# Two-layer graph attention on one core: filling order of a two-bank accumulator, a paired last sum, and a moved transpose

## The chip, the core and the metric

The kernel runs on one core of a Trainium2 chip. The metric is the device time of one execution in microseconds (us), as the median of several runs. TensorE (PE) does the matrix multiplications and the transposes, VectorE (DVE) and ScalarE (ACT) the elementwise work, GpSimd (POOL) one addition per block, and SyncE (SP) issues all transfers.

## The reference

For each of 32 graphs of 512 nodes, a layer norm and a ReLU are followed by two graph attention layers, and their result is added to the input:

```python
h = jnp.maximum(_layernorm(x, axis=-1), 0.0)
x = x + gnn(adj, h, ...)

def gat_layer(x, mask, W, a_src, a_dst, bias, concat):
    xl = (x @ W).reshape(B, N, H, F)
    asrc = jnp.einsum('bnhf,hf->bnh', xl, a_src)
    adst = jnp.einsum('bnhf,hf->bnh', xl, a_dst)
    e = leaky_relu(asrc[:, :, None, :] + adst[:, None, :, :], 0.2)
    e = jnp.where(mask[..., None], e, NEG_INF)
    attn = softmax(e, axis=1)
    out = jnp.einsum('bsdh,bshf->bdhf', attn, xl)
```

Layer 1 has 4 heads of 256 features (joined, with bias and ELU behind them), layer 2 has one head of 512. Everything is float32 but the masks. x is (32, 512, 512), adj (32, 512, 512) int32.

## The kernel before, in words

The 512 nodes of a graph are four blocks of 128 rows. The order of TensorE's instructions is the order of the program (`manual_schedule` for PE); the other engines' instructions are put in order by a list scheduler, which takes what it believes ready, by place in the program. Each engine then runs its own list strictly in that order.

One pass of the main loop (index `i`) takes four stages on TensorE, each on another graph:

- `project1(i+1)`: x @ W1, eight accumulators `pxl` of two banks (L279 to L287), each copied out by ACT (L286). Between them stand `turned_masks` (L177, L180), and, behind the fourth and fifth accumulator, layer 1's `columns` and `rows` for heads 0 and 1.
- `gather2(i-1)`: the last sum of layer 2 (L350 to L366): for each of four blocks `d` a load of x, an addition of the bias by POOL (L356), four matmuls into one bank of `ps` (L360), an addition by DVE (L364) and a store (L365). Two blocks share a two-bank accumulator.
- `project2(i)`: h1 @ W2, four accumulators `pxm` (L331, L338).
- `gather1(i+1)`: the weighted sums of layer 1 (L294 to L313): for each head `h` one accumulator `po` of two banks, `ps[:, f, :]` with `f` 0 and 1. Each half takes four matmuls (L301) and is then evicted: ACT exp (L308), DVE min (L309), DVE bias and max (L310). The half is evicted before the next half is filled.

All these accumulators share one ring of three two-bank buffers (tag "mm", bufs=3). Transposes use another ring of two (tag "tp").

The softmax of a head is the class `Soft`: `columns` copies its columns; `rows` turns them on TensorE (`pas`, L196) and spreads them over all partitions by two transfers through DRAM (L200, L202); `first` makes the row sums (ACT L232, DVE L235, ACT L239, ACT L242, and DVE L243 to L246, which write `r`); `turn` does for `r` what `rows` does for the columns (`prr`, L196, L200, L202); `second` makes the weights `p` (DVE L261, ACT L265, DVE L269). Layer 1 has four such chains; a table `plan` says behind which step of `gather2` and `project2` each part is issued. Layer 2's chain is called `late`. Before, its `rows` and `first` are issued behind the first half of `gather1`, its `turn` behind the sixth half, and its `second` behind the first accumulator of the next `project1`.

In the traces one matmul of float32 shows as two records, so a half of `po` is 8 records, `gather1` 64 and `gather2` 32.

Of the kernel before, what the change touches and what calls it, by code (L numbers as in the profile page):

```python
# [8 lines left out]
F32 = mybir.dt.float32  # L9
# [3 lines left out]
OP = mybir.AluOpType  # L13
# [3 lines left out]
P = 128  # L17
# [11 lines left out]
def tile_gat(  # L29
# [23 lines left out]
    nc = tc.nc  # L53
    B, N, D = x.shape
    H, FH = as1.shape
    HF = H * FH
    DO = w2.shape[1]
    NT = N // P
    KT = D // P
    FT = HF // P  # L60
    FPH = FH // P
# [4 lines left out]
    work = ctx.enter_context(tc.tile_pool(name="work", bufs=2))  # L66
    psum = ctx.enter_context(tc.tile_pool(name="psum", bufs=1, space=PSUM))
# [18 lines left out]
    b2_sb = const.tile([P, DO], F32, name="b2_sb")  # L86
# [36 lines left out]
    def load(b):  # L123
        XT[b] = []
        for t in range(NT):
            xt = work.tile([P, D], F32, tag="x", name=f"x{b}_{t}", bufs=4)
            nc.sync.dma_start(xt, x[b, t * P : (t + 1) * P, :])
            XT[b].append(xt)

    def load_adj(b):  # L130
        ADJ[b] = []
        for t in range(NT):
            a = work.tile([P, N], I32, tag="adj", name=f"adj{b}_{t}", bufs=2)
            nc.sync.dma_start(a, adj[b, t * P : (t + 1) * P, :])
            ADJ[b].append(a)

    def norm(b):

        stats = work.tile([P, NT, nc.vector.BN_STATS_DIM], F32, tag="stats", name=f"stats{b}")
        mv = work.tile([P, NT, nc.vector.BN_AGGR_DIM], F32, tag="mv", name=f"mv{b}")  # L140
        for t in range(NT):
            nc.vector.bn_stats(stats[:, t, :], XT[b][t])  # L142
            nc.vector.bn_aggr(mv[:, t, :], stats[:, t, :])
        rstd = work.tile([P, NT], F32, tag="rstd", name=f"rstd{b}")
        nc.vector.tensor_scalar_add(rstd, mv[:, :, 1], EPS)
        nc.gpsimd.tensor_tensor(rstd, rstd, half, op=OP.pow)
        yield
        HT[b] = work.tile([P, KT, N], F32, tag="ht", name=f"ht{b}", bufs=1)
        for t in range(NT):
            hn = work.tile([P, D], F32, tag="hn", name=f"hn{b}_{t}")  # L150
            nc.vector.tensor_scalar(  # L151
                hn, XT[b][t], mv[:, t, 0:1], rstd[:, t : t + 1], op0=OP.subtract, op1=OP.mult
            )
            ps = psum.tile([P, KT, P], F32, tag="tp", name=f"pht{b}_{t}", bufs=2)
            for k in range(KT):
                nc.tensor.transpose(ps[:, k, :], hn[:, k * P : (k + 1) * P], identf)
            nc.scalar.activation(HT[b][:, :, t * P : (t + 1) * P], ps, AF.Relu)
            yield
        del XT[b]
# [134 lines left out]
    def gather1(b):  # L294
        H1[b] = work.tile([P, FT, N], F32, tag="h1", name=f"h1{b}", bufs=1)
        for h in range(H):
            p = PS1.pop((b, h))
            ps = psum.tile([P, 2, 512], F32, tag="mm", name=f"po{b}_{h}", bufs=3)
            for f in range(FPH):
                for s in range(NT):  # L300
                    nc.tensor.matmul(  # L301
                        ps[:, f, :], xl[:, s, h, 2 + f * P : 2 + (f + 1) * P], p[:, s, :],
                        start=(s == 0), stop=(s == NT - 1),
                    )
                g = h * FPH + f
                bias = b1_sb[:, g : g + 1]
                e = work.tile([P, N], F32, tag="et", name=f"e{b}_{g}", bufs=2)
                nc.scalar.activation(e, ps[:, f, :], AF.Exp, bias=bias)  # L308
                nc.vector.tensor_scalar(e, e, 1.0, -1.0, op0=OP.min, op1=OP.add)  # L309
                nc.vector.scalar_tensor_tensor(  # L310
                    H1[b][:, g, :], ps[:, f, :], bias, e, op0=OP.add, op1=OP.max
                )
                yield  # L313

    def x2(b):

        if b < B - 1:
            return xl2

        return bass.AP(  # L320
            tensor=xl.tensor, offset=xl.offset, ap=[xl.ap[0], [DO + 2, NT], [1, DO + 2]]
        )
# [27 lines left out]
    def gather2(b):  # L350
        p = PS2.pop(b)
        v = x2(b)
        for d in range(NT):
            xr = work.tile([P, D], F32, tag="xr", name=f"xr{b}_{d}", bufs=3)
            nc.sync.dma_start(xr, x[b, d * P : (d + 1) * P, :])
            nc.gpsimd.tensor_tensor(xr, xr, b2_sb, op=OP.add)  # L356
            if d % 2 == 0:
                ps = psum.tile([P, 2, 512], F32, tag="mm", name=f"po2{b}_{d}", bufs=3)
            for s in range(NT):
                nc.tensor.matmul(  # L360
                    ps[:, d % 2, :], p[:, s, d * P : (d + 1) * P], v[:, s, 1 : DO + 1],
                    start=(s == 0), stop=(s == NT - 1),
                )
            nc.vector.tensor_tensor(xr, ps[:, d % 2, :], xr, op=OP.add)  # L364
            nc.sync.dma_start(out[b, d * P : (d + 1) * P, :], xr)  # L365
            yield  # L366

    def step(g):

        if g is not None:  # L370
            next(g, None)

    def rest(g):
        for _ in g or ():
            pass
# [7 lines left out]
    late = None  # L383
    with tc.manual_schedule(engines={mybir.EngineType.PE}):
        for i in range(-1, B + 1):

            front = i + 2 < B
            nm = norm(i + 2) if front else None
            if front:
                load(i + 2)  # L390
                load_adj(i + 2)
                step(nm)
            s1 = None
            if i + 1 < B:
                s1 = Soft(i + 1, 1, cols1, lambda h, p, b=i + 1: PS1.__setitem__((b, h), p))
                mt = turned_masks(i + 1)
                for n, _ in enumerate(project1(i + 1)):
                    if n == 0 and late:
                        late.second(0)
                    step(mt)  # L400
                    if n == 3:
                        s1.columns(0)
                    if n == 4:
                        s1.rows(0)
                    if n == 5:
                        s1.first(0)
                    if n == 7:
                        s1.columns(1)
                        s1.first(1)
            elif late:  # L410
                late.second(0)
            late = None
            last = i == B - 1
            stages = [gather2(i - 1)] if i >= 1 else []
            if 0 <= i < B:
                stages.insert(0 if last else 1, project2(i))

            plan = {
                1: lambda: s1.rows(1),
                3: lambda: (s1.turn(0), s1.first(2)),  # L420
                4: lambda: s1.second(0),
                6: lambda: (s1.turn(1), s1.first(3)),
                7: lambda: s1.second(1),
                8: lambda: s1.turn(2),
                9: lambda: s1.second(2),
                10: lambda: s1.turn(3),
                11: lambda: s1.second(3),
            }
            n = 0
            for g in stages:  # L430
                for _ in g:
                    n += 1
                    if s1 and n in plan:
                        plan.pop(n)()
                    if n in (2, 5, 7, 9):
                        step(nm)
                    if last and n == 8:
                        late = Soft(i, 2, cols2(i), lambda h, p, b=i: PS2.__setitem__(b, p))
                        late.columns(0)
                        late.rows(0)  # L440
                        late.first(0)
                    if last and n == 12:
                        late.turn(0)
            if s1:
                for n in sorted(plan):
                    plan.pop(n)()
            rest(nm)
            if 0 <= i < B and not last:
                late = Soft(i, 2, cols2(i), lambda h, p, b=i: PS2.__setitem__(b, p))
                late.columns(0)  # L450
            if i + 1 < B:
                for n, _ in enumerate(gather1(i + 1)):
                    if n == 0 and late:
                        late.rows(0)
                        late.first(0)
                    if n == 5 and late:
                        late.turn(0)
                    if n == 4 and front:
                        masks(i + 2)

# [28 lines left out]
```

## Time and profile before

| | before |
|---|---|
| median of 3 runs | 4053.54 us (4049.14 to 4060.91) |
| the profiled execution: its time, its span | 4057.44 us, 4055.7 us |
| PE busy | 3482.1 us (86%) |
| DVE busy | 2075.8 us (51%) |
| ACT busy | 1754.1 us (43%) |
| POOL busy | 230.0 us (6%) |
| mean granted TensorE clock | 0.936 of full speed |

Times in the rows below are microseconds from the start of the span, where a row begins with a time. A row of a timeline has the start, the duration, the engine, the line, the operation, what it writes and reads, and in brackets the idle time of the engine before it with what ended it.

### The profile page before, as it was taken

Reading aid. Unit: us, or ns where it says so; the run is one execution under the profiler, and the core shown is the slowest. Engines: PE = TensorE matmul, PEld = TensorE weight load, DVE = VectorE, ACT = ScalarE, POOL = GpSimd, SP = SyncE. Lnnn points to the kernel's source line nnn. Section 1 sums busy time; section 2 is a strip of 40 time slices with the busy share of each in tenths; the row PEclk is TensorE's granted clock in tenths of the full one; section 3 lists DMA queues with packets and bytes.
Section 4 is the critical chain, followed back from the end, with each engine's and each line's share of the span. In section 5 each row is a group of like instructions: output and inputs, shape, how many; then the busy total and the mean of one; then the engine's idle time right before and its main releaser. Section 6 shows DMA issues by size and latency. Waiting matters only on the chain.

```text
span 4055.7 us, 35993 instructions
## 1 busy us (share of the span) xinstructions
PE 3482.1 (86%) x12544; PEld 2278.3 (56%) x12544; DVE 2075.8 (51%) x4739; ACT 1754.1 (43%) x3489; POOL 230.0 (6%) x166
## 2 busy tenths in 40 slices
PE   4888889888889888898888988888988889888887
PEld 3655556555566455665555665546645556555564
DVE  7454555445554455554455544555544555445452
ACT  4443444443444335444344444344443444434451
POOL 0000000000000000000000000000000000000000
PEclk7999999999899899999999999999999999989999
DMA  5121222111222112221122221122211222111111
GB/s 166 34 69 48 75 67 81 65 58 55 70 76 71 50 57 70 76 79 58 47 76 66 81 69 64 50 65 76 79 57 47 73 68 81 63 46 59 60 55 47
DMA packets 120390, 269.41 MB, mean 66 GB/s; under 512 B 15504, under 2 KB 20496, under 8 KB 120208
## 3 DMA queue, kind: packets, MB, share of 16 engines
q1 hardware_dynamic: 120208, 267.12, 20.3%
q8 instruction: 98, 1.61, 0.2%
q14 instruction: 84, 0.69, 0.1%
HBM read 232.53 MB, written 34.54 MB: 66 GB/s over the span
## 4 chain that ended last, share of the span: by engine, by line
PE 45%; DVE 25%; ACT 15%; DMA 12%; issue 2%; POOL 1%; SPq 0%; DVEq 0%; POOLq 0%; ACTq 0%
PE po L301 22%; PE pxl L282 16%; DVE p L261 7%; DVE p L269 6%; ACT l L239 6%; PE po L360 5%; ACT l L232 5%; DMA oas<-das 4%; DMA orr<-drr 4%; DVE l L235 3%; DVE h L310 2%; DMA x<-in_x_dram 2%; ACT e L308 2%; DVE xr L364 1%; DVE hn L151 1%
## 5 line engine op out<-in xcount | busy, mean ns | idle before, releaser
L301 PE MATMUL po<-p,xl 128*128 128x512 f32 x2048 | 1109.5, 699 | 345.2 <-DVE h L310 345.2
L301 PEld LDWEIGHTS po<-p,xl 128*128 128x128 f32 x2048 | 444.0, 224 | 964.5 <-issue 528.8
L282 PE MATMUL pxl<-w_sb,ht 128*128 128x258 f32 x4096 | 931.8, 384 | 2.4 <-DMA adj<-in_adj_dram 1.6
L331 PE MATMUL pxm<-w_sb,h 128*128 128x257 f32 x4096 | 920.9, 379 | 0.0
L282 PEld LDWEIGHTS pxl<-w_sb,ht 128*128 128x128 f32 x4096 | 767.0, 190 | 126.5 <-issue 14.8
L331 PEld LDWEIGHTS pxm<-w_sb,h 128*128 128x128 f32 x4096 | 761.5, 189 | 130.1 <-issue 11.1
L235 DVE CUSTOM_DVE_ANT_0 l<-l,mt 128x512 f32<-128x512 f32 x640 | 432.1, 703 | 383.3 <-ACT l L232 383.3
L265 ACT ACTIVATE p<-p,lo 128x512 f32<-128x512 f32 x640 | 426.3, 716 | 450.7 <-DVE p L261 450.7
L308 ACT ACTIVATE e<-po,b_sb 128x512 f32<-128x512 f32 x256 | 174.9, 683 | 891.0 <-PE po L301 891.0
L360 PE MATMUL po<-xl,p 128*128 128x512 f32 x1024 | 472.7, 604 | 83.3 <-DVE xr L364 71.5
L239 ACT ACTIVATE l<-l,low 128x512 f32<-128x512 f32 x640 | 454.2, 711 | 87.4 <-DVE low L235 86.8
L232 ACT ACTIVATE l<-oas,sc 128x512 f32<-128x512 f32 x640 | 426.6, 710 | 97.5 <-DMA oas<-das 97.5
L261 DVE SCALAR_TENSOR_TENSOR p<-orr,lo 128x512 f32<-128x512 f32 x640 | 442.0, 752 | 49.4 <-DMA orr<-drr 49.4
L309 DVE TENSOR_SCALAR e<-e 128x512 f32<-128x512 f32 x256 | 108.7, 425 | 644.6 <-ACT e L308 644.6
L286 ACT ACTIVATE xl<-pxl 128x516 f32<-128x516 f32 x256 | 151.3, 597 | 612.8 <-PE pxl L282 612.6
L269 DVE TENSOR_TENSOR p<-p,m 128x1024 f32<-128x1024 f32 x320 | 402.2, 1275 | 4.9 <-ACT p L265 4.7
L356 POOL TENSOR_TENSOR xr<-xr,b_sb 128x512 f32<-128x512 f32 x128 | 196.7, 1537 | 3453.4 <-DMA xr<-in_x_dram 2858.1
L360 PEld LDWEIGHTS po<-xl,p 128*128 128x128 f32 x1024 | 188.4, 191 | 314.7 <-issue 201.3
L310 DVE SCALAR_TENSOR_TENSOR h<-po,b_sb,e 128x512 f32<-128x512 f32 x256 | 191.3, 747 | 5.9
L180 DVE TENSOR_SCALAR mt<-pm 128x512 bf16<-128x512 bf16 x128 | 54.3, 424 | 267.3 <-PE pm L177 267.3
L142 DVE BATCH_NORM_STATS2 stats<-x 128x6 f32<-128x512 f32 x128 | 87.4, 684 | 129.5 <-DMA x<-in_x_dram 129.5
L198 DVE COPY rrr<-prr 8x128 f32<-8x128 f32 x160 | 43.4, 271 | 162.5 <-PE prr L196 162.5
(43 smaller groups left out, 1174.9 us busy)
## 6 DMA issues: line engine op xcount, KB each, us to landing
orr<-drr SPq DMA_DIRECT2D x160, 512.0 KB
x<-in_x_dram SPq DMA_DIRECT2D x128, 256.0 KB
adj<-in_adj_dram SPq DMA_DIRECT2D x128, 256.0 KB
xr<-in_x_dram SPq DMA_DIRECT2D x128, 256.0 KB
oas<-das SPq DMA_DIRECT2D x64, 512.0 KB
out_dram<-xr SPq DMA_DIRECT2D x128, 256.0 KB
oas<-das SPq DMA_DIRECT2D x32, 256.0 KB
drr<-rrr SPq DMA_DIRECT2D x160, 4.0 KB
```

Of the source, the lines that this page charges most:

```text
L232: nc.scalar.activation(e, self.asr[i][:, j, :], AF.Prelu, bias=ad[:, d : d + 1], alpha=SLOPE)
L235: nc.vector.tensor_tensor_reduce(out=e, in0=e, in1=MASKT[self.b][:, d, :], scale=-1.0, scalar=BIG, op0=OP.add, op1=OP.min, accum_out=low[: ...
L239: nc.scalar.activation(e, e, AF.Exp, bias=low[:, d : d + 1], scale=-1.0, accum_out=tot[:, d : d + 1])
L261: nc.vector.scalar_tensor_tensor(p[:, u, :], rr[:, 0, :], lo[:, 0, j, u : u + 1], rr[:, 1, :], op0=OP.add, op1=OP.max,)
L265: nc.scalar.activation(p[:, u, :], p[:, u, :], AF.Exp, bias=lo[:, 1, j, u : u + 1])
L269: nc.vector.tensor_tensor(pp, pp, MASK[self.b][:, t : t + 2, :], op=OP.min)
L282: nc.tensor.matmul(ps[:, j, :W], ht[:, k, t * P : (t + 1) * P], w1_sb[:, k, hp + j, :], start=(k == 0), stop=(k == KT - 1),)
L301: nc.tensor.matmul(ps[:, f, :], xl[:, s, h, 2 + f * P : 2 + (f + 1) * P], p[:, s, :], start=(s == 0), stop=(s == NT - 1),)
L308: nc.scalar.activation(e, ps[:, f, :], AF.Exp, bias=bias)
L310: nc.vector.scalar_tensor_tensor(H1[b][:, g, :], ps[:, f, :], bias, e, op0=OP.add, op1=OP.max)
L331: nc.tensor.matmul(ps[:, j, : W - 1], h1[:, k, t * P : (t + 1) * P], w2_sb[:, k, j * (W - 1) : (j + 1) * (W - 1)], start=(k == 0), stop=(k ...
L360: nc.tensor.matmul(ps[:, d % 2, :], p[:, s, d * P : (d + 1) * P], v[:, s, 1 : DO + 1], start=(s == 0), stop=(s == NT - 1),)
```

## The change

Three things are altered. In `gather1` both halves of a head are filled first, and then both are evicted; a step of the loop (`yield`) still stands behind each half. In `gather2` two blocks share one load tile (two buffers of two blocks, in place of three of one), one POOL addition over both, one DVE addition over both, and two stores behind it. In layer 2's chain, `rows` and `first` are issued behind the third half of `gather1` (step 2) instead of the first, and `turn` behind the first accumulator of the next `project1`, right before `second`, instead of behind the sixth half of `gather1`.

```diff
@@ gather1
                     )
+                if f < FPH - 1:
+                    yield
+            for f in range(FPH):
                 g = h * FPH + f
...
                 )
-                yield
+            yield
@@ gather2
-        for d in range(NT):
-            xr = work.tile([P, D], F32, tag="xr", name=f"xr{b}_{d}", bufs=3)
-            nc.sync.dma_start(xr, x[b, d * P : (d + 1) * P, :])
-            nc.gpsimd.tensor_tensor(xr, xr, b2_sb, op=OP.add)
-            if d % 2 == 0:
-                ps = psum.tile([P, 2, 512], F32, tag="mm", name=f"po2{b}_{d}", bufs=3)
-            for s in range(NT):
-                nc.tensor.matmul(
-                    ps[:, d % 2, :], p[:, s, d * P : (d + 1) * P], v[:, s, 1 : DO + 1],
-                    start=(s == 0), stop=(s == NT - 1),
-                )
-            nc.vector.tensor_tensor(xr, ps[:, d % 2, :], xr, op=OP.add)
-            nc.sync.dma_start(out[b, d * P : (d + 1) * P, :], xr)
+        for d in range(0, NT, 2):
+            xr = work.tile([P, 2, D], F32, tag="xr", name=f"xr{b}_{d}", bufs=2)
+            for j in range(2):
+                nc.sync.dma_start(xr[:, j, :], x[b, (d + j) * P : (d + j + 1) * P, :])
+            nc.gpsimd.tensor_tensor(
+                xr, xr, b2_sb[:, None, :].to_broadcast([P, 2, D]), op=OP.add
+            )
+            ps = psum.tile([P, 2, 512], F32, tag="mm", name=f"po2{b}_{d}", bufs=3)
+            for j in range(2):
+                for s in range(NT):
+                    nc.tensor.matmul(
+                        ps[:, j, :], p[:, s, (d + j) * P : (d + j + 1) * P], v[:, s, 1 : DO + 1],
+                        start=(s == 0), stop=(s == NT - 1),
+                    )
+                if j == 0:
+                    yield
+            nc.vector.tensor_tensor(xr, ps, xr, op=OP.add)
+            for j in range(2):
+                nc.sync.dma_start(out[b, (d + j) * P : (d + j + 1) * P, :], xr[:, j, :])
             yield
@@ main loop, project1
                     if n == 0 and late:
+                        late.turn(0)
                         late.second(0)
...
             elif late:
+                if i < B:
+                    late.turn(0)
                 late.second(0)
@@ main loop, gather1
-                    if n == 0 and late:
+                    if n == 2 and late:
                         late.rows(0)
                         late.first(0)
-                    if n == 5 and late:
-                        late.turn(0)
```

## Rows read from the trace of the kernel before

**Rows 1.** Stages of one pass: length, PE, PEld, DVE, ACT, POOL busy, clock, DMA, GB/s.

```profile
1993.83:2022.90 29.07, 29.07 (x146) 25.04 (x145) 8.83 (x24) 9.25 (x18) 0.00 (x0) 1.00 0.18 55
2022.90:2039.77 16.87, 14.94 (x39) 6.46 (x38) 10.28 (x35) 13.58 (x32) 3.32 (x2) 1.00 0.38 129
2039.77:2069.25 29.48, 29.48 (x145) 25.43 (x143) 23.00 (x45) 15.60 (x32) 4.09 (x3) 1.00 0.34 117
2069.25:2116.82 47.57, 34.48 (x68) 13.88 (x67) 22.09 (x44) 16.30 (x30) 0.00 (x0) 0.86 0.07 21
```

**Rows 2.** Waits of PE: us in total, times, longest.

```profile
PE po L301 <- DVE h L310: 345.2, 128, 8.5
...
PE po L360 <- DVE xr L364: 71.5, 64, 3.3
```

**Rows 3.** Timeline of PE in gather1 of that pass.

```profile
2069.25 3.60 PE L301 MATMUL po<-p,xl 128*128 128x512 f32 x8
2075.39 0.37 PE L196 MATMUL pas<-identf,sc 128*4 128x128 f32 x1 [2.54 <-DVE sc L345]
2077.83 9.20 PE L301 MATMUL po<-p,xl 128*128 128x512 f32 x16 [2.06 <-DVE h L310]
2091.45 8.83 PE L301 MATMUL po<-p,xl 128*128 128x512 f32 x16 [4.43 <-DVE h L310]
...
2107.55 0.27 PE L196 MATMUL prr<-identf,r 128*8 128x128 f32 x1
2107.65 3.60 PE L301 MATMUL po<-p,xl 128*128 128x512 f32 x8
```

**Rows 4.** Timeline of PE in gather2 of that pass.

```profile
2022.90 3.60 PE L360 MATMUL po<-xl,p 128*128 128x512 f32 x8
2026.34 0.27 PE L196 MATMUL pas<-identf,sc 128*8 128x128 f32 x1
...
2031.41 0.60 PE L156 MATMUL pht<-identf,hn 128*128 128x128 f32 x4
2031.84 3.60 PE L360 MATMUL po<-xl,p 128*128 128x512 f32 x8
```

**Rows 5.** Sum over the stretches of all 32 gather1 stages, columns as in rows 1.

```profile
sum 1545.76, PE 1113.82 PEld 449.32 DVE 734.49 ACT 531.01 POOL 1.01; mean PE 34.81 PEld 14.04 DVE 22.95 ACT 16.59 POOL 0.03
```

**Rows 6.** Sum over gather2 of the 30 passes with all four stages.

```profile
sum 519.38, PE 451.30 PEld 194.52 DVE 305.44 ACT 408.06 POOL 91.27; mean PE 15.04 PEld 6.48 DVE 10.18 ACT 13.60 POOL 3.04
```

**Rows 7.** Timeline of DVE around gather1: weights of heads 2, 3, layer 2's r, weights.

```profile
2069.02 2.35 DVE L269 TENSOR_TENSOR p<-p,m 128x1024 f32<-128x1024 f32 x2
...
2075.15 1.23 DVE L269 TENSOR_TENSOR p<-p,m 128x1024 f32<-128x1024 f32 x1
...
2091.39 0.15 DVE L246 SCALAR_TENSOR_TENSOR r<-sc,low 128x4 f32<-128x4 f32 x1
...
2115.79 2.35 DVE L269 TENSOR_TENSOR p<-p,m 128x1024 f32<-128x1024 f32 x2
```

**Rows 8.** Groups by line: count, busy us, mean ns, idle before.

```profile
L364 DVE TENSOR_TENSOR xr<-po,xr 128x512 f32<-128x512 f32 x128 | 88.3, 690 | 71.8 <-PE po L360 59.1 <-issue 8.9 <-POOL xr L356 3.1
L356 POOL TENSOR_TENSOR xr<-xr,b_sb 128x512 f32<-128x512 f32 x128 | 196.7, 1537 | 3453.4 <-DMA xr<-in_x_dram 2858.1 <-DVE hn L151 500.2 <-DVE low L235 65.6
```

**Rows 9.** Timeline of POOL and DVE where POOL's addition runs.

```profile
2041.21 1.31 POOL L356 TENSOR_TENSOR xr<-xr,b_sb 128x512 f32<-128x512 f32 x1 [1.89 <-DMA xr<-in_x_dram]
2041.32 1.23 DVE L245 TENSOR_TENSOR r<-sc,low 128x4 f32<-128x4 f32 x1
```

**Rows 10.** Timeline of DVE in the next project1: last mask operation, then columns.

```profile
2123.10 0.43 DVE L167 TENSOR_TENSOR m<-m,diag 128x512 bf16<-128x512 bf16 x1
...
2132.41 0.18 DVE L290 COPY sc<-xl 128x16 f32<-128x16 f32 x1
```

**Rows 11.** Timeline of SP in gather2: a store and the load behind it.

```profile
2027.84 0.34 SPq L365 DMA_DIRECT2D out_dram<-xr  x1
...
2029.87 0.33 SPq L355 DMA_DIRECT2D xr<-in_x_dram  x1
```

## The prediction, made before the changed kernel was seen

> **What bounds the kernel now.** I read the stages of one pass first [rows 1]. Three of the four stages run at the full clock, and in project1 and project2 TensorE is busy for the whole stretch (29.07 of 29.07 us, 29.48 of 29.48). DVE and ACT never reach the length of a stage, so TensorE's order is the path. The exception is gather1: 47.57 us long, 34.48 us busy, granted clock 0.86. Next come TensorE's waits [rows 2]: 345.2 us for L310, 128 times, which is once for each of 4 heads in 32 graphs, and 71.5 us for L364. The timeline of gather1 shows where they fall [rows 3]: the first half of a head takes 8 records, then TensorE stands until DVE has written the head's first half (2.06 us, 4.43 us and the like), and then runs 16 records, the second half and the next head's first half, in one go. So it is never the next head that waits, only the other bank of the same accumulator. Behind each wait the 16 records take 9.20 or 8.83 us, though 8 at full clock need 3.44: some of them run at 1.2 GHz instead of 2.4. One more wait belongs to this change: `pas`, 2.54 us for layer 2's columns [rows 3].
>
> **What gather1 costs without the wait.** Eight records start to the next instruction take 2026.34 − 2022.90 = 3.44 us [rows 4], 0.43 each; a small transpose adds 2107.65 − 2107.55 = 0.10 [rows 3]. 64 records and the one transpose that stays (`pas`) are 27.52 + 0.10 = 27.62 us, against 47.57. Over 32 graphs the stage takes 1545.8 us [rows 5]; 32 × 27.62 = 883.8; the gain is 662.0 us. It holds both terms, idle time and the slow clock behind it, since the stage then follows project2, which ran at full clock without a gap [rows 1].
>
> The eviction of a pair is as much work as before, only later. A half took about 2.0 us behind its last matmul (the shortest waits), a pair, one after the other, at most twice that, 4.1 us. Nobody waits for it soon: the ring has three buffers, so head 3 reuses head 0's buffer, which is filled by 6.9 us and needed at 20.7 us. I cost it at nothing; if that cover were gone, each us past it would be a us per graph.
>
> **Gather2.** 32 records (13.76), two small transposes (0.20) and one group of four (0.43, from 2031.41 to 2031.84) make 14.39 us [rows 3, 4]. The 30 stages take 519.4 us [rows 6]; 30 × 14.39 = 431.7; the gain is 87.7 us. DVE's addition over 1024 columns lies between 0.69 (one L364) and 1.38 us (two); L269 has that shape and takes about 1.2 [rows 7, 8]; it frees a buffer needed two accumulators later, 7 us, so nothing on the path. POOL's addition lies between 1.5 and 3.1 us [rows 8]; I take the upper end, and POOL has most of the pass free [rows 1]. On SP the same loads and stores are issued, in pairs: a load waits there for the store that frees its tile, 2.0 us in the trace [rows 11], now twice a pass instead of up to four times. Layer 1's transfers queue behind it, 0 to 2 us; their cover is below. At the very end the last eviction is 0.5 us longer and one more store follows; the two last gathers lose their own waits of a us or so each. I set the end at zero, within ±3.
>
> **The moved chain of layer 2.** `pas` now comes behind the third half, 10.3 us into gather1. Its columns were there at 2075.4, 6.1 us in, so its wait goes. From `pas` to `r` took 2091.54 − 2075.39 = 16.2 us [rows 3, 7]; lower bound 14, since ACT stood there for a head; upper 17.6, with two more exps of 0.69 in between. I take 16.2: `r` at 26.5. The turn stands behind the first accumulator of project1, at 27.6 + 3.5 = 31.1: 4.6 us to spare, so the wait that the program adds there costs nothing. If it did, the whole of project1 is queued behind it on TensorE. From `prr` to the last weights took 2118.14 − 2107.55 = 10.6 us (start of L269 2115.79 + 2.35) [rows 3, 7]; so `p` is ready at 41.7, 14 us into project1, and gather2 asks for it 29.2 us in: 15 us of cover. The turn moves 0.10 us from gather1 (where it is already left out) into project1: 30 × 0.10 = 3.0 us back.
>
> Behind `second` DVE does a later graph's masks, 2118.14 to 2123.53, 5.4 us with the loads they free on SP [rows 7, 10]. They shift to 14 to 19.5 us into project1. DVE's columns of layer 1 (L290) ran 15.6 us in [rows 10] and `pas` of layer 1 asks for them at 18.6. If the whole mask group goes ahead of them, TensorE waits 1 us; if it does not, nothing. I take nothing and keep 30 us for the range.
>
> **Is the shorter pass still TensorE's?** A pass shrinks from 123.0 to 29.17 + 14.39 + 29.48 + 27.62 = 100.7 us; DVE's 64.2 and ACT's 54.7 us (sums over the four rows) fit [rows 1]. The tightest chain is head 2 of layer 1: weights done at 2071.37 [rows 7], asked for 13.9 us into gather1, and gather1 starts 2.5 us earlier: 2069.25 − 2.5 + 13.9 = 2080.7; 9.3 us to spare. Head 3: 2076.38 against 2087.5.
>
> A POOL addition holds up DVE: an operation on four columns took 1.23 us while one ran [rows 9], against 0.15 for its neighbour of the same size [rows 7]. With pairs a single hold can reach 3.1 us, twice a pass; with the 2 us of SP that is at most 8 us late, inside the 9.3. The Trainium skill speaks against the pairing here (SBUF — State Buffer, Who interferes with whom): a DVE instruction with two SBUF inputs contends with a GpSimd instruction that reads SBUF, and the other side blocks for the whole instruction. By that rule the hold lengthens as POOL's instruction does, and the sum stays as it is as long as the spare time does.
>
> **The sum.** 662.0 + 87.7 − 3.0 = 746.7; 4055.7 − 746.7 = 3309.0 us of span, 3310.7 with the 1.7 us around it. The profiled execution lies 3.9 us over the median, which gives 3307; the first graphs start gather1 behind idle time and so in part at the low clock even then, about 2 us each. Forecast: 3310 us.
>
> **Rivals.** (A) The forecast, all waits gone: 3310. Chance 0.64.
>
> (B) A new wait on TensorE in project1, for `r` at the turn or for L290 behind the masks. For: both are now in TensorE's order with 3 to 5 us to spare, and the list scheduler may put ACT's exps of heads 2 and 3, which wait for TensorE, ahead of `first`. Against: even `r` held until head 3 is done (27.6) is before 31.1 but for its last small steps. 1 to 3 us per pass, 30 passes: 3340 to 3400. Chance 0.20.
>
> (C) The layer-1 chain runs out of its 9.3 us, with DVE as the bound of the stretch before gather1. For: gather2 and project2 are where DVE is densest, and POOL's and SP's delays add to up to 8 us. Against: it needs all of them at once. 2 to 5 us past the cover in 30 passes: 3370 to 3460. Chance 0.10.
>
> (D) The change does not do what it says: the wait for L310 is not for the eviction of the other bank, and a fill of the second half stays behind something DVE does. Then nothing moves, 4050. Against: the wait ends with L310 each time and the next head's half never waits. The Trainium skill (PSUM — Partial Sum Buffer, PSUM bank collisions raise a hardware error) has engines in different banks run cleanly side by side; by that rule the wait is one the program sets for the whole accumulator, which the new order satisfies. Chance 0.03.
>
> (E) Slower. `r` comes late at the turn, since ACT works strictly in order and `first` lands behind exps and copies that wait for project1's matmuls, which stand behind the turn's wait. Place: `prr` in project1. Price: a us per pass for each us that `r` is past 31.1, and slower records behind the gap (16 took 2 us more [rows 3]). It outweighs the gain, 746.7/30 = 24.9 us per pass, once `r` comes 22.9 us after the turn is reached (22.9 + 2), 54 us after the start of gather1 instead of 26.5; at 58 the time would be 4054 + 30 × 4 = 4174. Chance 0.03.
>
> **How the numbers follow.** The range 3295 to 3430 holds A with its small bounds (±3 at the end, the start of the first graphs, 3 per mille of the whole), B, and C's nearer half; C's far end, D and E, about 0.1, are left out. Differences under 0.3%, 12 us, could not be told from no change: A, B and C are all faster, 0.94; D is the same, 0.03; E slower, 0.03.
>
> **What would show it.** Right: gather1 of a pass 27 to 28 us with granted clock 1.00; no wait of PE for L310 or L364 but in the first and last graphs; gather2 14.4 us; a pass of about 101 us. B would show as idle time before `prr` or `pas` in project1, C as waits of L301 for L269, D as waits for L310 of the old size. The forecast is wrong if a pass of the middle is over 103 us.

## The result and the profile after

| | before | after |
|---|---|---|
| median of 4 runs each | 4051.34 us (4046.82 to 4060.91) | 3345.03 us (3343.32 to 3347.70) |
| the profiled execution: its time, its span | 4057.44, 4055.7 us | 3347.70, 3345.9 us |
| mean granted TensorE clock | 0.936 | 0.989 |

After against before is 0.8255, with a 95% interval of 0.8238 to 0.8271. The forecast was 3310 us: the sign and most of the size came, and 35 us of the gain did not.

The page of the changed kernel, busy time of each engine:

```profile
PE 3244.2 (97%) x12544; PEld 2221.7 (66%) x12544; DVE 2128.6 (64%) x4675; ACT 1748.3 (52%) x3489; POOL 228.3 (7%) x102
```

TensorE is now busy for 97% of the span instead of 86%, in 238 us less busy time for the same 12544 instructions: that is the slow clock behind the old waits, the mean granted clock being 0.989 instead of 0.936. The stages of one pass in the middle, in the order and with the columns of [rows 1]:

```profile
1945.88:1975.06 29.18, 29.18 (x148) 25.13 (x147) 13.40 (x30) 10.66 (x19) 0.00 (x0) 1.00 0.23 73
1975.06:1989.47 14.41, 14.41 (x39) 6.46 (x38) 9.13 (x31) 12.91 (x32) 0.00 (x0) 1.00 0.32 105
1989.47:2019.88 30.41, 29.64 (x144) 25.35 (x143) 23.79 (x44) 15.73 (x33) 6.81 (x3) 1.00 0.34 124
2019.88:2047.46 27.58, 27.58 (x67) 12.16 (x65) 19.70 (x40) 15.11 (x28) 0.00 (x0) 1.00 0.09 29
```

Read them against the forecast stage by stage: project1 29.18 (29.17 foretold), gather2 14.41 (14.39), gather1 27.58 (27.62) at clock 1.00, and in these three TensorE is busy for the whole stretch. project2 is the odd one: 30.41 us long and 29.64 busy, where it had been 29.48 without a gap. The pass is 101.58 us. The sums of the three stages over the kernel (32 gather1, 32 project2, 30 gather2; the first and the last answer to [rows 5] and [rows 6]):

```profile
sum 885.99, PE 885.99 PEld 390.63 DVE 614.91 ACT 471.41 POOL 1.08; mean PE 27.69 PEld 12.21 DVE 19.22 ACT 14.73 POOL 0.03
...
sum 978.08, PE 946.34 PEld 810.00 DVE 756.71 ACT 515.23 POOL 214.20; mean PE 29.57 PEld 25.31 DVE 23.65 ACT 16.10 POOL 6.69
...
sum 432.76, PE 432.14 PEld 193.53 DVE 260.80 ACT 374.71 POOL 0.00; mean PE 14.40 PEld 6.45 DVE 8.69 ACT 12.49 POOL 0.00
```

gather1 gave 1545.76 − 885.99 = 659.8 us, gather2 519.38 − 432.76 = 86.6. project2, 946.46 us in the kernel before, took 31.6 back; project1 took 0.11 in each of 30 passes, 3.3. The balance is 711.5 us; 4055.7 − 711.5 = 3344.2, 1.7 short of the measured span.

TensorE's waits, columns as in [rows 2]:

```profile
PE prr L196 <- DVE rrr L198: 26.2, 27, 1.8
PE prr L196 <- DVE r L246: 20.1, 4, 7.3
PE po L366 <- DVE p L269: 14.6, 1, 14.6
```

Both waits of [rows 2] are gone from the list. The second and third line belong to the first and last graphs, where the kernel before has them too. The first is new: 27 times, about 1 us each, a turn of `r` waiting for the copy of the turn before it. The timeline of TensorE in gather1 and at the moved turn, answering to [rows 3]:

```profile
2019.88 10.46 PE L301 MATMUL po<-p,xl 128*128 128x512 f32 x24
2030.18 0.27 PE L196 MATMUL pas<-identf,sc 128*4 128x128 f32 x1
2030.29 17.33 PE L301 MATMUL po<-p,xl 128*128 128x512 f32 x40
2047.46 3.64 PE L282 MATMUL pxl<-w_sb,ht 128*128 128x258 f32 x16
2050.94 0.27 PE L196 MATMUL prr<-identf,r 128*8 128x128 f32 x1
```

24 and 40 records run as one stretch each, with `pas` between them at 10.3 us and no bracket of idle time anywhere; `prr` behind the first accumulator of project1 waits for nothing either.

### The profile page after: what moved, and what is told of

It is laid out like the page before. It is cut to its first block, busy times and chain, and to the rows that moved or that the text cites. A ratio compares the mean times of both kernels' runs of the same rounds, so it can differ in the third digit from the quotient of the medians.

```text
span 3345.9 us, 35756 instructions
## 1 busy us (share of the span) xinstructions
PE 3244.2 (97%) x12544; PEld 2221.7 (66%) x12544; DVE 2128.6 (64%) x4675; ACT 1748.3 (52%) x3489; POOL 228.3 (7%) x102
## 4 chain that ended last, share of the span: by engine, by line
PE 67%; DVE 18%; DMA 8%; ACT 4%; issue 1%; POOL 1%; SPq 0%; POOLq 0%; ACTq 0%; DVEq 0%
PE po L301 26%; PE pxl L282 20%; PE pxm L334 10%; PE po L366 9%; DVE p L261 5%; DVE l L235 5%; DVE p L269 3%; DMA oas<-das 2%; DMA x<-in_x_dram 2%; ACT l L232 2%; ACT l L239 2%; DMA orr<-drr 2%; DMA das<-ras 1%; DVE hn L151 1%; DMA adj<-in_adj_dram 1%
## 5 line engine op out<-in xcount | busy, mean ns | idle before, releaser
L301 PE MATMUL po<-p,xl 128*128 128x512 f32 x2048 | 891.1, 594 | 0.0
L235 DVE CUSTOM_DVE_ANT_0 l<-l,mt 128x512 f32<-128x512 f32 x640 | 532.9, 861 | 499.2 <-ACT l L232 498.2
L301 PEld LDWEIGHTS po<-p,xl 128*128 128x128 f32 x2048 | 388.0, 191 | 474.2 <-issue 454.6
L366 PE MATMUL po<-xl,p 128*128 128x512 f32 x1024 | 459.3, 595 | 14.6 <-DVE p L269 14.6
L269 DVE TENSOR_TENSOR p<-p,m 128x1024 f32<-128x1024 f32 x320 | 385.9, 1224 | 2.9 <-ACT p L265 2.9
L360 POOL TENSOR_TENSOR xr<-xr,b_sb 128x1024 f32<-128x1024 f32 x64 | 194.9, 3046 | 2818.6 <-DMA xr<-in_x_dram 2450.4
L239 ACT ACTIVATION_READ_ACCUMULATOR l<-l,low 128x1 f32 x640 | 120.5, 188 | 0.0
```

The source lines that it names most:

```text
L235: nc.vector.tensor_tensor_reduce(out=e, in0=e, in1=MASKT[self.b][:, d, :], scale=-1.0, scalar=BIG, op0=OP.add, op1=OP.min, accum_out=low[: ...
L239: nc.scalar.activation(e, e, AF.Exp, bias=low[:, d : d + 1], scale=-1.0, accum_out=tot[:, d : d + 1])
L269: nc.vector.tensor_tensor(pp, pp, MASK[self.b][:, t : t + 2, :], op=OP.min)
L301: nc.tensor.matmul(ps[:, f, :], xl[:, s, h, 2 + f * P : 2 + (f + 1) * P], p[:, s, :], start=(s == 0), stop=(s == NT - 1),)
L360: nc.gpsimd.tensor_tensor(xr, xr, b2_sb[:, None, :].to_broadcast([P, 2, D]), op=OP.add)
L366: nc.tensor.matmul(ps[:, j, :], p[:, s, (d + j) * P : (d + j + 1) * P], v[:, s, 1 : DO + 1], start=(s == 0), stop=(s == NT - 1),)
```

## The experiments

The time of each kernel is a median, its ratio is against the kernel before, with the 95% interval. Five of them take the change apart (eviction order, pairing, moves, and the change without one or the other), one asks what the old wait was for, and the rest go after the 35 us. A deletion or an addition in a diff is against the kernel before for the first four, against the changed kernel from the fifth on.

### Only the order of filling and eviction

```diff
+                if f < FPH - 1:
+                    yield
+            for f in range(FPH):
                 g = h * FPH + f
...
-                yield
+            yield
```

> The kernel before with the new eviction order alone (both halves of a head filled, then both evicted); gather2 and layer 2's turns as before. Theory (the wait for the other bank was the whole loss of gather1): the stage falls from 47.6 us to about 33 us: 27.7 us of matmuls, 2.5 us of wait for layer 2's columns at the first small transpose, up to 1 us of wait for r at the turn, and some slow records behind these waits; gather2 keeps its 16.9 us; time 3540 to 3600 us. Rival (the moves carry part of the gain, because the turn now stands in front of a late r): the stage stays at 36 us or more, over 3650 us. Rival (the wait is not for the other bank): no change, 4050 us.

Measured: 3518.72 us, 0.8687 (0.8668 to 0.8705). This part alone brings 533 of the 706 us, and the time lies 21 us under what was expected. Its waits of TensorE:

```profile
PE pas L196 <- DVE sc L348: 84.0, 31, 5.1
PE po L363 <- DVE xr L367: 74.7, 64, 3.6
```

No wait for the other bank is left. What is left is layer 2's columns (`pas`, behind the first half as before, where it waited 87.6 us) and the last sum's addition. The sum of its gather1 is 994.4 us, 31 a graph, a little better than expected.

### A tile of its own for each half, evicted half by half as before

```diff
-            ps = psum.tile([P, 2, 512], F32, tag="mm", name=f"po{b}_{h}", bufs=3)
             for f in range(FPH):
+                ps = psum.tile([P, 2, 512], F32, tag="mm", name=f"po{b}_{h}_{f}", bufs=3)
...
-                        ps[:, f, :], xl[:, s, h, 2 + f * P : 2 + (f + 1) * P], p[:, s, :],
+                        ps[:, 0, :], xl[:, s, h, 2 + f * P : 2 + (f + 1) * P], p[:, s, :],
```

> The kernel before, with a tile of its own for each half of a head in gather1 (one bank of a two-bank buffer of the same ring), evicted after each half as before. Theory (the program makes the second half wait because it belongs to the same tile, although it lies in another bank): the waits of L301 for L310 mostly vanish without any change of order, gather1 falls to 32 to 36 us, time 3560 to 3680 us. Rival (a matmul cannot fill while ACT or DVE evict, or the order itself is what counts): the waits stay, over 3900 us.

Measured: 3523.07 us, 0.8693 (0.8671 to 0.8715), better than expected and within 5 us of the kernel above. Its waits:

```profile
PE pas L196 <- DVE sc L345: 83.7, 31, 5.0
PE po L360 <- DVE xr L364: 74.7, 64, 4.6
```

The second half here is filled while the first is evicted, in the old order, and TensorE does not stand for it. So the eviction was never too slow, and the wait went with the tile: half an accumulator in a tile of its own is not waited for. That kills rival (D) and agrees with the Trainium skill (PSUM — Partial Sum Buffer, PSUM bank collisions raise a hardware error), which has engines in different banks run side by side. One thing is argued and not shown: each half now takes a buffer of the ring, so the second half lies in another pair of banks, and no run fills the second bank of a pair while its first is evicted.

### Only the pairing of the last sum

```diff
+        for d in range(0, NT, 2):
+            xr = work.tile([P, 2, D], F32, tag="xr", name=f"xr{b}_{d}", bufs=2)
...
```

(the whole of the diff's part for `gather2`, nothing else)

> The kernel before with the paired last sum alone. Theory: gather2 falls from 16.9 us (mean 17.3) to 14.4 us in 30 passes, 80 to 90 us in all: 3960 to 3970 us, with the waits of gather1 unchanged. Rival (the longer POOL addition holds DVE so that the time comes back in project2 or gather1): 4000 us or more.

Measured: 4020.02 us, 0.9918 (0.9902 to 0.9935): 31 us, not the 88 of the forecast's term. The rival was right. gather2 did fall by the 87 us, to 432.0 in its 30 stages, and the waits say where the rest went:

```profile
PE po L301 <- DVE h L310: 296.7, 128, 8.5
PE pas L196 <- DVE sc L346: 141.8, 29, 5.9
PE prr L196 <- DVE rrr L198: 38.9, 28, 2.0
```

The wait for the last sum is gone from the list, but the new wait for `rrr` appears with the pairing alone, 38.9 us, and its project2 sums to 990.5 us, 44.0 over before. The wait for `pas` is 141.8 us, 87.6 before. So the residue of the changed kernel belongs to the pairing.

### Only the moves of layer 2's chain

```diff
                     if n == 0 and late:
+                        late.turn(0)
                         late.second(0)
...
-                    if n == 0 and late:
+                    if n == 2 and late:
                         late.rows(0)
                         late.first(0)
-                    if n == 5 and late:
-                        late.turn(0)
```

> The kernel before with layer 2's rows, first and turn moved as in the change, and nothing else. Theory: the moves only pay where the wait for the other bank is gone; the first wait of gather1 ends with ACT's exps of head 3 in any case, and the hold of the fourth half by first only moves to a later half: 4020 to 4070 us. Rival (the moves are worth their 2.5 us wait and more per graph by themselves): under 3980 us.

Measured: 4060.60 us, 1.0021 (1.0006 to 1.0035), as expected. The `pas` wait went, but the wait of L301 for L310 rose from 345.2 to 401.5 us and that of L360 for L364 from 71.5 to 93.4. gather1 sums to 1497.5 us, 48 less than before, and gather2 to 571.8 in its 30 stages, 52 more.

### The change without the pairing

The `gather2` of before in the changed kernel.

> The changed kernel with the paired last sum undone (eviction order and moved turns stay). Theory (the pairing brings the new wait in project2 with it): gather2 back at 16.9 us and more, project2 at 29.5 us without its wait of a us, gather1 27.6 us; 3400 to 3420 us, so the pairing nets 55 to 75 us of the 88 us that gather2 gained. Rival (the wait in project2 comes from the shorter pass as such): project2 stays at 30.4 us and the time is 3430 to 3440 us.

Measured: 3389.04 us, 0.8356 (0.8334 to 0.8377), some 11 us under the lower end. project2 is 29.48 us again, without a wait; L363 waits 60.2 us for L367. Against the changed kernel the pairing therefore nets 44.0 us, less than the 55 to 75 expected. gather2 sums to 506.9 us here and to 432.8 there, project2 to 947.9 and 978.1: a gain of 74.1 less a cost of 30.2. gather2 gains less than 86.6 because its wait is already smaller here than in the kernel before (60.2 against 71.5).

### The change without the moves

`rows` and `first` behind the first half, `turn` behind the sixth, as before.

> The changed kernel with layer 2's rows, first and turn where they were (behind the first and the sixth half of gather1); eviction order and pairing stay. Theory (the moves take away the wait for layer 2's columns and the slow records behind it, which the eviction order alone left at 3.5 us of gather1): gather1 at 31 to 32 us, 3455 to 3485 us, so that the moves are worth 110 to 140 us here though they were worth nothing on the kernel before. Rival (the pairing already shifts DVE so far that the moves matter less): under 3430 us.

Measured: 3564.36 us, 0.8796 (0.8779 to 0.8813): missed by 80 us, and 46 us worse than the eviction order alone. gather1 sums to 1087.6 us, 34 a graph where 31 to 32 were expected. Its waits, and its timeline of TensorE in one gather1:

```profile
PE pas L196 <- DVE sc L349: 137.1, 29, 5.5
PE prr L196 <- DVE rrr L198: 39.0, 28, 2.6
```

```profile
1939.33 0.37 PE L196 MATMUL pas<-identf,sc 128*4 128x128 f32 x1 [4.82 <-DVE sc L349]
1939.50 19.37 PE L301 MATMUL po<-p,xl 128*128 128x512 f32 x40
```

Here the paired sum makes gather2 shorter and the columns later, so `pas` waits 4.7 us on average (137.1/29), 2.7 in the kernel with the eviction order alone (84.0/31). And the wait is dearer than its length: 40 records behind the 4.82 us take 19.37 us at a granted clock of 0.89, where they take 17.33 at 1.00 in the changed kernel. With the pairing in place the moves are worth 3564 − 3345 = 219 us; without it 3519 − 3389 = 130 us. Neither figure is the price of a part by itself: alone the moves brought nothing (1.0021) and the pairing 31 us.

### Half the addition at a time on POOL

```diff
-            nc.gpsimd.tensor_tensor(
-                xr, xr, b2_sb[:, None, :].to_broadcast([P, 2, D]), op=OP.add
-            )
+            for j in range(2):
+                nc.gpsimd.tensor_tensor(xr[:, j, :], xr[:, j, :], b2_sb, op=OP.add)
```

> The changed kernel with POOL's addition over two blocks split into two of one block each; everything else stays paired. Theory (the long POOL addition holds a DVE instruction for about 2 us, twice a pass, and so the copy of the third turn is late): each hold is shorter, PE's wait for that copy falls from 26 us to under 10 us, 3318 to 3332 us. Rival (TensorE is just 2.5 us earlier at the fourth turn, as gather2 is shorter, and DVE is as late as it was): no change, 3340 to 3348 us.

Measured: 3335.23 us, 0.8224 (0.8202 to 0.8247). The direction is the theory's, the size a little less: the wait falls from 26.2 us to this, and project2 to 961.9.

```profile
PE prr L196 <- DVE rrr L198: 11.3, 16, 1.6
```

All 4675 instructions of DVE and all 3489 of ACT come in the same order as in the changed kernel, so nothing but the addition differs. The halves still hold DVE: it is busy for 2111.7 us against 2128.6 in the changed kernel, and L151, which ran almost free there (70.1 us), now falls under them too (93.7).

### No addition of layer 2's bias

```diff
-            nc.gpsimd.tensor_tensor(
-                xr, xr, b2_sb[:, None, :].to_broadcast([P, 2, D]), op=OP.add
-            )
```

> The changed kernel without POOL's addition (the bias of layer 2 is left out). Theory (POOL's hold of DVE): without it the wait for the copy of the third turn is gone, project2 is back at 29.5 us, 3308 to 3320 us. Rival (TensorE earlier, DVE as late as it was): the wait stays at half or more of its 26 us, 3330 to 3348 us.

Measured: 3311.00 us, 0.8165 (0.8144 to 0.8185). The wait for `rrr` is gone, project2 is 29.48, and the time is the forecast's. Here too DVE and ACT have all their instructions in the order of the changed kernel, so the scheduler has no part in it. Every other term of the sum has thereby come out as foretold; 34 of the 35 us hang on this instruction.

### The same addition on DVE

```diff
-            nc.gpsimd.tensor_tensor(
+            nc.vector.tensor_tensor(
```

> The changed kernel with the bias of layer 2 added by DVE instead of POOL (the same operation over two blocks). Theory (what makes the third turn's copy late is POOL holding a DVE instruction, about 3.6 us per pass, not DVE's amount of work): DVE does 2.4 us more per pass in the open, nothing is held, and the wait falls to under 10 us: 3312 to 3328 us. Rival (DVE is simply full there): 3338 to 3355 us.

Measured: 3311.78 us (3311.36 to 3313.31), 0.8172 (0.8157 to 0.8187), just under the lower end of what was expected. **This kernel beats both**, by 33 us the changed one. DVE has the work of 64 additions more, is busy for less time (2076.9 us against 2128.6), and TensorE waits less, so it is not DVE's load that delayed the copy but what POOL did to it. The lines of DVE's row sums and of the addition, first in the changed kernel:

```profile
L235 DVE CUSTOM_DVE_ANT_0 l<-l,mt 128x512 f32<-128x512 f32 x640 | 532.9, 861 | 499.2 <-ACT l L232 498.2
L360 POOL TENSOR_TENSOR xr<-xr,b_sb 128x1024 f32<-128x1024 f32 x64 | 194.9, 3046 | 2818.6 <-DMA xr<-in_x_dram 2450.4 <-DVE xr L372 338.2 <-DVE p L261 20.1
```

and with the addition on DVE:

```profile
L235 DVE CUSTOM_DVE_ANT_0 l<-l,mt 128x512 f32<-128x512 f32 x640 | 421.0, 687 | 462.1 <-ACT l L232 461.4
L360 DVE TENSOR_TENSOR xr<-xr,b_sb 128x1024 f32<-128x1024 f32 x64 | 77.8, 1217 | 0.4
```

The same 640 row sums take 112 us less. Done by DVE the addition costs 77.8 us of DVE; done by POOL it takes 194.9 us of POOL and holds DVE for 121 (2128.6 busy, 2007.7 without any addition), 112 of them in these row sums. Without any addition L235 takes 420.8, with the halves 495.5. All of DVE counted, the hold is 0 us without the addition, 104 with the halves and 121 in the changed kernel, and TensorE's wait for `rrr` none, 11.3 and 26.2.

How the hold reaches TensorE, from the timelines of both engines and POOL in project2 of the changed kernel, which begins at 1989.47:

```profile
1991.09 2.62 POOL L360 TENSOR_TENSOR xr<-xr,b_sb 128x1024 f32<-128x1024 f32 x1 [84.47 <-DMA xr<-in_x_dram]
1991.42 2.85 DVE L235 CUSTOM_DVE_ANT_0 l<-l,mt 128x512 f32<-128x512 f32 x1
...
1999.06 3.18 POOL L360 TENSOR_TENSOR xr<-xr,b_sb 128x1024 f32<-128x1024 f32 x1 [5.35 <-DMA xr<-in_x_dram]
2000.14 2.65 DVE L235 CUSTOM_DVE_ANT_0 l<-l,mt 128x512 f32<-128x512 f32 x1
...
2011.35 1.22 DVE L269 TENSOR_TENSOR p<-p,m 128x1024 f32<-128x1024 f32 x1
2012.49 0.27 DVE L198 COPY rrr<-prr 8x128 f32<-8x128 f32 x1
2012.81 0.27 PE L196 MATMUL prr<-identf,r 128*8 128x128 f32 x1 [0.77 <-DVE rrr L198]
```

The same copy and turn with the addition on DVE; project2 begins with the first row:

```profile
1970.52 3.64 PE L334 MATMUL pxm<-w_sb,h 128*128 128x257 f32 x16
...
1981.27 1.21 DVE L360 TENSOR_TENSOR xr<-xr,b_sb 128x1024 f32<-128x1024 f32 x1
...
1990.46 0.27 DVE L198 COPY rrr<-prr 8x128 f32<-8x128 f32 x1
...
1992.93 0.27 PE L196 MATMUL prr<-identf,r 128*8 128x128 f32 x1
```

Twice in this pass an L235 takes 2.65 to 2.85 us instead of 0.69, having begun while POOL's addition ran; each ends about 0.55 us behind POOL's end (1994.27 against 1993.71, 2002.79 against 2002.24), as if it had begun only then. In the whole kernel 55 of the 640 take 1.97 to 2.89 us, and every one of them began behind an addition's start and ends 0.55 us behind its end. The copy of the third turn comes 23.02 us into project2 in the changed kernel (2012.49 − 1989.47) and 19.94 without the hold (1990.46 − 1970.52). The next turn, the fourth of the pass, needs a buffer of the small ring of two ("tp"). Without the hold the copy has ended 1990.46 + 0.27 = 1990.73 and the turn comes at 1992.93: 2.2 us of cover. The delay of 3.1 us eats them, and TensorE stands for 0.77 us. Over 25 middle passes the medians are 23.1 us in the changed kernel and 20.6 here, with 1.6 us of cover left here.

Against the kernel before, DVE is not later. Counted from the start of gather2 (medians of the same passes), the copy comes after 37.9 us in the kernel before, 37.5 in the changed kernel, 35.0 with the addition on DVE and 34.5 without it. TensorE is earlier: it reaches the fourth turn after 39.3 us before and after 36.8 here, since gather2 is 2.5 us shorter. The cover was 1.4 us before, and the pairing took more than that. So the wait has two conditions, the shorter gather2 and the hold that keeps DVE from following; the change without the pairing lacks the first, this kernel the second, and neither waits.

### The bias in the copy of layer 2's products

The bias is added where `pxm` is copied out, by DVE instead of ACT's copy, and the addition in `gather2` falls away; the bias tile is widened by two zero columns (not shown).

```diff
-            nc.scalar.activation(
-                v[:, t, :].rearrange("p (c w) -> p c w", c=2), ps[:, :, : W - 1], AF.Copy
+            nc.vector.tensor_tensor(
+                v[:, t, :].rearrange("p (c w) -> p c w", c=2), ps[:, :, : W - 1],
+                b2_sb.rearrange("p (c w) -> p c w", c=2), op=OP.add,
             )
```

> The changed kernel with the bias of layer 2 added where h1 @ W2 is copied out (the weights of a softmax sum to one), by DVE in place of ACT's copy, and no addition by POOL. Theory (POOL's hold is the residue): DVE has 2.8 us more per pass and ACT 2.3 us less, no hold: 3312 to 3330 us. Rival (DVE, strictly in order, now also lets the accumulators of project2 wait): 3335 us or more.

Measured: 3323.85 us, 0.8200 (0.8185 to 0.8216). The wait for `rrr` is gone here too, but not because the copy is earlier. Project2 begins with the first row, and the other two are the fourth turn and the copy of the third:

```profile
1974.79 3.64 PE L335 MATMUL pxm<-w_sb,h 128*128 128x257 f32 x16
...
1997.20 0.27 PE L197 MATMUL prr<-identf,r 128*8 128x128 f32 x1
1997.99 0.27 DVE L199 COPY rrr<-prr 8x128 f32<-8x128 f32 x1
```

The copy comes 23.2 us into project2, as late as in the changed kernel, and the turn ran before it. In the trace the fourth turn waits here for a semaphore of ACT and no longer for one of DVE: it got the other buffer of the small ring when the kernel was built. So this run says nothing of the hold. `pas` waits 5.8 us in all for layer 2's columns, and the time is 12 us behind the addition by DVE.

### The layer norm's last transposes two steps later

```diff
-                    if n in (2, 5, 7, 9):
+                    if n in (2, 5, 7, 11):
```

> The changed kernel with the last block's transposes of the layer norm issued behind step 11 instead of step 9, so that the fourth turn takes the other buffer of the small ring and no longer needs the third turn's copy; DVE's work is the same. Theory (the residue of the change is that one wait of TensorE, about 1 us in 27 passes, and nothing else): the wait is gone, project2 at 29.5 us, 3312 to 3322 us, whatever makes DVE late. Rival (DVE is late for all that follows, so the wait turns up at the next transposes or at the weights of gather1): 3335 to 3350 us.

Measured: 3365.14 us, 0.8298 (0.8276 to 0.8320). The theory fell. Its waits:

```profile
PE pas L196 <- DVE sc L290: 23.4, 27, 3.1
PE prr L196 <- DVE r L246: 20.1, 4, 7.3
PE pxl L282 <- DVE h L313: 14.6, 20, 2.0
```

The wait for `rrr` went from the list and project2 is back at 29.48 us, as the theory had it, but two other waits came: 19.4 of the 23.4 us of `pas` in gather2, for the columns of heads 2 and 3, and the wait of `pxl` in project1. Moving a group on TensorE made the scheduler put ACT's and DVE's lists in another order, and the kernel is 20 us slower than the changed one. How much of that is the order and how much is POOL's hold, met at a later place, is not shown. Here cover for one copy could not be bought by moving its neighbours alone.

### The addition on DVE, without the moves

> Eviction order and pairing of the change, the bias added by DVE instead of POOL, layer 2's rows, first and turn where they were before. Theory (the moves are worth what they take away of the wait for layer 2's columns; with POOL's hold DVE reaches these columns about 2 us later, so the moves cover a part of the hold): gather1 falls back from 34.7 to about 31 us and project2 to 29.5 us, 3405 to 3450 us, so that the moves are worth about 110 to 130 us here against 219 with POOL's addition. Rival (DVE is as late without the hold): gather1 stays at 34 us, over 3500 us.

Measured: 3473.00 us, 0.8569 (0.8553 to 0.8585), above the theory's upper end. Its main wait:

```profile
PE pas L196 <- DVE sc L349: 109.6, 29, 5.6
```

The hold is gone and so is the wait for `rrr`, which brings 91 us against the change without the moves. But `pas` still waits 3.8 us each time, longer than the 2.7 with the eviction order alone. So the hold is only part of why the pairing makes layer 2's columns late. The other part is again the shorter gather2. Counted from its start (medians of 25 middle passes), the columns are ready after 52.8 us with the eviction order alone and after 51.1 here, and gather1 starts after 46.4 and 43.9: DVE comes 1.7 us sooner, TensorE 2.5.

## Why the prediction came out as it did

**Gather1.** Right: 27.69 us a graph against 27.62, 659.8 against 662.0 us. The reading that only the other bank is ever waited for, and that this wait is the tile's bookkeeping, is borne out by the half tiles. The term holds two of the three parts: 1545.8 − 994.4 = 551 us come with the eviction order alone, the other 108 only once the moves take the wait for `pas` away.

**Gather2.** Right as a stage, 14.40 against 14.39 us. That nobody waits for a later addition of 1024 columns held: L372 takes 1217 ns, inside the bounds given.

**The moved chain.** Right: neither `pas` nor the moved `prr` waits, and project1 grew by 0.11 us. The feared wait for L290 behind the masks did not come in the changed kernel. With the later transposes it came for 4 us in project1; the rest of the 23.4 us was in gather2, for the columns of other heads.

**The hold by POOL: the step that failed.** I set its cost at nothing, since "with pairs a single hold can reach 3.1 us, twice a pass", and 8 us with SP's part would lie "inside the 9.3". The length of a hold was right (POOL's addition takes 3.05 us, the row sums under it 2.65 to 2.85), but I had taken the cover from one place, the weights of head 2 before gather1, and these were indeed never waited for. DVE's queue meets TensorE earlier: at the copy of the third turn, which frees a buffer of the small ring. Its cover in the kernel before was 1.4 us (median). The pairing brought TensorE there 2.5 us sooner, the hold kept DVE where it had been, and about 1 us of waiting was left in most passes. The prediction took the 2.5 us off the cover of head 2 and never asked for the cover of this copy. The term that was set at 0 measured 31.6 us in project2, which is 86% of the 36.9 us between the forecast span and the measured one; the others are 2.2 (gather1), 1.1 (gather2), 0.3 (project1) and 1.7 us (the ends). Without the addition the time is 3311.0.

The Trainium skill had the rule (SBUF — State Buffer, Who interferes with whom), and I had quoted it as speaking against the pairing: a DVE instruction with two SBUF inputs contends with a GpSimd instruction that reads SBUF, and the port pair that they share is an exclusive lock. The trace agrees, with 0.69 us stretched to 2.85. What was wrong was the cover set against it, not the rule.

**The rivals.** (B) had the size, 3340 to 3400, and named a wait on TensorE of 1 to 3 us a pass; it put it in project1, for `r` or L290, and it came in project2, for a buffer behind `rrr`. (C) had the cause, POOL's delays on DVE, but the chain that it named never ran out: L301 waits for L269 nowhere in the list. (D) is excluded by the half tiles. (E) did not happen: the turn has its `r` in time.

## What to carry to other kernels

A delay that a change puts on an engine's queue has to be held against the first instruction behind it that another engine waits for, small ones too: here a copy of 0.27 us that frees one of two buffers, not the large work at the end of the chain. Time that a change saves on one engine comes off the cover of all others: here 2.5 us against a cover of 1.4. An addition given to POOL to spare DVE may cost DVE more than doing it (121 us against 78), so price the hold before offloading. A wait that is gone from the list may have been moved to another buffer and not cured, so look at when the awaited instruction runs. And where a wait falls between two banks of one tile, try a tile for each bank or fill both first: either took the wait away.

## What the runs showed that I had not expected

- The parts do not add. Alone the pairing brings 31 us, on top of the eviction order it costs 46, and with eviction order and moves it brings 44. TensorE's idle time moves to the next late value as soon as a stage gets shorter.
- The addition split in two halves on POOL holds DVE for 104 us in all, against 121 in one piece, although POOL works as many elements: the row sums lose 37 us of their excess, and 24 us of it come back at L151.
- What a gap costs on the clock could not be read from its length. With the eviction order alone, 40 records behind a wait of 2.63 us took 19.03 us (granted clock 0.91) in one graph and 17.33 us, the full pace (1.00), in another; behind one of 3.00 us they took 17.33. In the change without the moves, waits of 3.28 to 5.47 us were followed by 18.69 to 20.19 us, the longest not by the most.

```profile
299.52 0.27 PE L196 MATMUL pas<-identf,sc 128*4 128x128 f32 x1 [2.63 <-DVE sc L348]
299.63 19.03 PE L301 MATMUL po<-p,xl 128*128 128x512 f32 x40
...
1803.15 0.27 PE L196 MATMUL pas<-identf,sc 128*4 128x128 f32 x1 [2.63 <-DVE sc L348]
1803.25 17.33 PE L301 MATMUL po<-p,xl 128*128 128x512 f32 x40
...
2015.71 0.27 PE L196 MATMUL pas<-identf,sc 128*4 128x128 f32 x1 [3.00 <-DVE sc L348]
2015.82 17.33 PE L301 MATMUL po<-p,xl 128*128 128x512 f32 x40
```
